# A four-layer graph network on one core: left-over rows on another queue, feature sums stored where they are made, entry counts moved by one sweep, and ties in the order of one queue

## The chip, the core and the metric

One core of a Trainium2 chip runs the whole program. The number that counts is the device time of one execution in microseconds (us); where runs are compared it is the median of several. Engines are named as the profile names them: PE is the matrix engine (PEld its weight loads), DVE the vector engine, ACT the scalar engine, POOL the general engine, SP the engine that here does nothing but issue transfers. A queue named SPq, ACTq or POOLq is the list of transfers that this engine issues, in order.

## The reference

A graph of 2708 nodes with 512 features and a dense matrix `adj` (2708 x 2708, float32, mostly zeros) goes through four layers. Each ends in a layer norm over the features:

```python
deg = jnp.maximum((adj != 0).sum(-1), 1.0)
x = layernorm(x + L0(x, adj))     # head = (adj > 0) / sqrt(count); inc = adj + head; (inc @ x) / sum(inc)
x = layernorm(x + L1(x, adj))     # gates from adj @ x; e = exp(-leaky_relu(s_left + s_right)) where adj != 0;
                                  # sigmoid(g_a * (e @ h) / sum(e) + g_b * (adj @ (x @ W) + b)), h = x @ W_sa
x = layernorm(x + L2(x, adj))     # x @ W0 + (A x) @ W1 + (A A x) @ W2 + (A A A x) @ W3
x = layernorm(x + L3(x, adj, deg))# relu((D^-1/2 (A + I) D^-1/2 x + x) @ W + b)
```

So `adj` is multiplied with a 2708 x 512 matrix seven times, in float32.

## The kernel before

**Seven sweeps over the matrix.** Each product with `adj` is one sweep. Sweep 0 is layer 0, sweep 1 makes `adj @ x` of layer 1, sweep 2 its attention product, sweeps 3 to 5 are the three hops of layer 2, and sweep 6 is layer 3. The nodes are split into two halves of 1354 and every sweep uses Strassen's seven block products (named P1 to P7 in sweeps 0 to 2, Q1 to Q7 in sweeps 3 to 6) on the blocks "11", "12", "21", "22" of the matrix and "B11" to "B22" of the features. The matrix blocks are combined by DVE (`comb`, line 419, and line 1382 in the later sweeps) into `s3` = 11 - 21, `s1` = 21 + 22, `s2` = s1 - 11, `s4` = 12 - s2; the feature blocks are combined into T1 to T4 (`x_sums` and `x_last`). Sweeps 0 to 2 go over four ranges of columns, 384, 384, 256 and 330 wide in sweeps 1 and 2; sweep 0 takes the 256 wide range first, as plain block products with no combining. Each half is ten blocks of 128 rows and 74 rows left over. `rest_adj` loads the left-over rows as a tile `r` of 116 rows and a tile `r32`, in which 32 rows stand four times.

**What sets the order.** The program is a list of pieces with positions: `at(pos, fn)` puts `fn` at a position, and the pieces are called in order of position. Sweep s begins at `S[s]` = 28 s, a range of sweeps 0 to 2 takes seven positions, and one position is one block product. From the list a scheduler then orders each engine's instructions by what it expects to be ready. A piece with `hold` keeps its place in the list, on all engines or on the one that is named. Until position 5 (`START`) the list holds throughout. [...]

**The pieces that the change touches.**

- *Start.* `count_mask` (lines 760 to 763) turns each matrix tile of the first range into zeros and ones, PE counts them (`cnt`, line 774), and a row `row` of one over the square root comes out (lines 795 to 814). `prep0` (lines 829 and 830) adds it to the tiles, and only then can the first product run. All loads of this range, `r` and `r32` among them, are on SP's queue.
- *Between sweeps 0 and 1.* `layernorm` has a step on POOL, a power (line 605), between two steps on DVE. Its result is stored to `X1` on POOL's queue and loaded again on POOL's queue as the features of sweep 1 (`next_x`, `x_load`, the loads at line 150).
- *Entry counts.* `extra1` counts the non-zero entries of each column for `deg`, tile by tile on DVE (`tally`, lines 1039 and 1042), in all four ranges of sweep 1. The counts lie in seven slots of one buffer, `masks`, which `sums2` later takes for weight sums.
- *Sweep 2's pairs.* `pairs2` finishes the nodes of a range during the next range, 128 nodes of both halves at a time: `b` is their dense product in two parts (`seven`, line 692), `c` a sigmoid on ACT, `e` the layer norm, `f` transposes both tiles (`ps_t`, line 642, `xT`), `z` makes the four sums S1 to S4 of the transposed tiles (`node_sums`, line 1193, names `d`), and `g` multiplies them. `f` and `g` hold their place on PE.
- *Added feature sums.* Sweep 3 multiplies features to the matrix's columns as two more blocks of rows. `ext_loads` loads the transposed features `X2T`, `ext_sums` (line 1344) makes their four sums on DVE and stores them to `SE` (`Es`, line 1345) on POOL's queue, in four parts for each of two column ranges g. Those of g = 0 run during sweep 2, at `S[2] + 19.3` and after, those of g = 1 during sweep 3. Their tiles come from the ring, 38 buffers that the matrix tiles, `e` tiles, sums and loads share.
- *Last sweep.* `done6` makes the dense product for finished columns (`row_sums`, line 682, then `seven`). `rest_add` (line 1519) adds the left-over rows' products `accr`, which take four of the eight accumulator banks.

Of the kernel before, what the change touches and what calls it, by code (L numbers as in the profile page):

```python
# [24 lines left out]
ALU = mybir.AluOpType  # L25
P = 128
EPS = 1e-5
NH = 1354
KT = 11
# [39 lines left out]
def gnn_kernel(ctx: ExitStack, tc: tile.TileContext, x, adjT, w_sa, a_sa, w_gcn, b_gcn, wab, bab, w_hop, w_out,  # L69
# [106 lines left out]
    events = []  # L176

    held = set()

    def at(pos, fn, hold=False):  # L180

# [68 lines left out]
    def x_load(src, k, s, eng):  # L250
# [2 lines left out]
        t = b12_tile(k) if s == "B12" else new_x(s, k)  # L253
        move(eng, t[:w], q)

    def next_x(base, src, sums=0.95, halves=-0.25):


        q = nc.gpsimd

        ql = nc.scalar if base == S[1] else q
        at(base + 1.3, lambda: rest_x(src, ql))
        for k in range(KW):
            f = k / KT
            if (k * P) < RANGES[-1][0]:
                at(base - 5.8 + f, lambda k=k: x_load(src, k, "B11", q))
                at(base - 1.85 + f, lambda k=k: x_load(src, k, "B22", q))
                at(base - 1.84 + f, lambda k=k: x_load(src, k, "B12", q))
                at(base + (0.03 if base == S[1] else -1.15) + f, lambda k=k: x_sums(k), True)
                at(base - 0.85 + f, lambda k=k: x_load(src, k, "B21", q))  # L270
                at(base + 1.5 + f, lambda k=k: x_last(k), True)
            else:
                at(base + halves + 0.05 * (k - 8), lambda k=k: x_load(src, k, "B22", ql))
                at(base + max(halves, 0.1) + 0.05 * (k - 8), lambda k=k: x_load(src, k, "B21", ql))
                at(base + sums + 0.03 * (k - 8), lambda k=k: x_sums(k), True)
                at(base + 2.6 + 0.03 * (k - 8), lambda k=k: x_last(k), True)
# [19 lines left out]
            rows_over(q, groups[s, "R"][0], (lo[:, c], hi[:, c]))  # L296
            q.dma_start(out=t32[64 * e : 64 * e + 64], in_=copies(hi[KA - KR :, c], 2))

    def rest_adj(h, R0, n):
        t, t32 = ring_tile("r"), ring_tile("r32")  # L300
        a = adjT[:, h * NH + R0 : h * NH + R0 + n]
        rows_over(nc.sync, t[:, :n], (a[NH - KR : NH], a[2 * NH - KR :]))
        nc.sync.dma_start(out=t32[:, :n], in_=copies(a[2 * NH - 32 :], 4))
        return t, t32

    REST_HOMES = [("B11", "B22"), ("B21", "T1")]
# [82 lines left out]
    def sweep(base, ranges, prep=None, extra=None, done=None, first=False, late=None, sums=False, save=False):  # L389
        A, spare = {}, {}  # L390
        nk = KW
        for r, (R0, n) in enumerate(ranges):
# [45 lines left out]
                        p, f = pw[ij]  # L438
                        at(pb + p + f * k / nk, lambda ij=ij, k=k, prepare=prepare: prepare(ij, k))

            def rest_load(h, R0=R0, n=n, r=r):
                A[r, "r", h], A[r, "r32", h] = rest_adj(h, R0, n)

            def rest_prepare(h, R0=R0, n=n, r=r):
                prep(R0, n, h, NT, KA, A[r, "r", h])
# [6 lines left out]
            for k in ks if not plain else ():  # L452
                f = 0.75 * k / nk
                at(pb + cw["s3"] + f, lambda k=k, comb=comb: comb("s3", "11", "21", ALU.subtract, k))
                at(pb + cw["s1"] + f, lambda k=k, comb=comb: comb("21", "21", "22", ALU.add, k))
                at(pb + cw["s2"] + f, lambda k=k, comb=comb: comb("11", "21", "11", ALU.subtract, k))
                at(pb + cw["s4"] + f, lambda k=k, comb=comb: comb("11", "12", "11", ALU.subtract, k))
                if sums:
                    at(pb + cw["s1"] + 0.95 + f, lambda k=k, run=run: run(1, k))
                    at(pb + cw["s4"] + 0.15 + f, lambda k=k, run=run: run(0, k))  # L460
# [137 lines left out]
    def layernorm(dsts, y, w, on_scalar=False, late=None):  # L598
        st = small.tile([P, 6], F32, name="st")
        nc.vector.bn_stats(st[:w], y[:w])  # L600
        mv = small.tile([P, 2], F32, name="mv")
        nc.vector.bn_aggr(mv[:w], st[:w])
        rstd = small.tile([P, 2], F32, name="rstd")
        nc.vector.tensor_scalar(rstd[:w, 0:1], mv[:w, 1:2], EPS, None, ALU.add)  # L604
        nc.gpsimd.tensor_tensor(rstd[:w, 1:2], rstd[:w, 0:1], neg_half[:w], ALU.pow)  # L605
        if on_scalar:
            nc.vector.scalar_tensor_tensor(rstd[:w, 0:1], mv[:w, 0:1], -1.0, rstd[:w, 1:2], ALU.mult, ALU.mult)
        for d, c0, c1 in dsts:
            if on_scalar:
                fn = lambda d=d, c0=c0, c1=c1: nc.scalar.activation(d[:w], y[:w, c0:c1], AF.Identity,  # L610
                                                                    bias=rstd[:w, 0:1], scale=rstd[:w, 1:2])
                fn() if late is None else late.append(fn)
                continue
            nc.vector.tensor_scalar(d[:w], y[:w, c0:c1], mv[:w, 0:1], rstd[:w, 1:2], ALU.subtract, ALU.mult)
# [414 lines left out]
    at(S[1] + 2.33 + 0.95 * (i - 1), scores_over)  # L1029

    def extra1(pb, r, R0, n, A):
        ts = tiles_of(R0, n)

        def tally(h, key, w=P):

            a = A[(r,) + key]
            if (R0, h) not in deg:
                deg[R0, h] = d = mask_tile()
                nc.vector.tensor_scalar(d[:w, :n], a[:w, :n], 0.0, None, ALU.not_equal)
            else:  # L1040
                d = deg[R0, h]
                nc.vector.scalar_tensor_tensor(d[:w, :n], a[:w, :n], 0.0, d[:w, :n], ALU.not_equal, ALU.add)  # L1042

        for ij, p in (("11", -0.6), ("21", 0.05), ("22", 1.05), ("12", 3.6)):
            for k in range(KW):
                at(pb + p + 0.8 * k / KT, lambda ij=ij, k=k: tally(int(ij[0]) - 1, (ij, k)), r == 0)
        for h, p in ((1, 2.0), (0, 4.5)):
            at(pb + p, lambda h=h: tally(h, ("r", h), KA))
            at(pb + p, lambda h=h: tally(h, ("r32", h), 32))

        def end(h):
            d = deg.pop((R0, h))
            ps = bank("ds", [P, 4])
            for i, q in enumerate(ts):
                wq = wt(q)
                nc.tensor.matmul(ps[:wq, i : i + 1], d[:, q * P - R0 : q * P - R0 + wq], ones_bf[:, 0:1], start=True,
                                 stop=True)
            for i, q in enumerate(ts):
                wq = wt(q)
                o = rdeg[:wq, h * KT + q : h * KT + q + 1]  # L1060
                nc.vector.tensor_scalar(o, ps[:wq, i : i + 1], 1.0, None, ALU.max)
                nc.vector.tensor_scalar(diag[:wq, h, q : q + 1], o, 1.0, None, ALU.add)
                nc.vector.reciprocal(o, o)

        def rows(h):
            to_rows(rdeg[:, h * KT + ts[0] : h * KT + ts[-1] + 1], len(ts),
                    DROW[h][0, ts[0] * P : (ts[-1] + 1) * P].rearrange("(k i) -> k i", i=P))

        at(pb + 2.6, lambda: end(1))
        at(pb + 3.7, lambda: rows(1))  # L1070
        at(pb + 5.2, lambda: end(0))
        at(pb + 6.3, lambda: rows(0))
# [78 lines left out]
            o, w = (W[2][2 * c + 1], w_sa) if k == 2 else (W[3][c][:, HD:], w_hop[3])  # L1151
            nc.scalar.dma_start(out=o, in_=w[c * P : (c + 1) * P, HD:])

    at(S[2] + 6.4, sums2)
    at(S[2] + 23.4, lambda: again(2))
    at(S[2] + 24.2, lambda: again(3))

# [9 lines left out]
    def extra2(pb, r, R0, n, A):  # L1167
# [7 lines left out]
        def share(o, s, t, w):  # L1175
            nc.vector.tensor_scalar(o, s, 1e-5, None, ALU.add)
            nc.vector.reciprocal(o, o)
            nc.vector.tensor_tensor(o, o, gate[:w, t, 0:1], ALU.mult)

        at(pb - 1.6, lambda: rows(0))  # L1180
        at(pb - 1.0, lambda: rows(1))
        at(pb + 5.2, lambda: run_sums(R0, n, 0, share))
# [2 lines left out]
    def node_sums(x, y):  # L1185
# [5 lines left out]
        for m, o, p, q, op in (("S3", r[0], a11, a21, ALU.subtract), ("S1", r[1], a21, a22, ALU.add),  # L1191
                               ("S2", r[2], r[1], a11, ALU.subtract), ("S4", r[3], a12, r[2], ALU.subtract)):
            nc.vector.tensor_tensor(o, p, q, op)
            Z.update({(m, c): o[:, c, :] for c in range(2)})
        for m, o in (("A11", a11), ("A12", a12), ("A22", a22)):
            Z.update({(m, c): o[:, c, :] for c in range(2)})
# [2 lines left out]
    def pairs2(p0, R0, n, C, tiles):  # L1199
        Y = {}  # L1200
        at(p0 + 0.2, lambda: Y.update(row_sums({(i, c): C[1 - i, c] for i in range(2) for c in range(DC)}, n)))
        for i, (t0, lo, w) in enumerate(tiles):
# [22 lines left out]
            def f(j, lo=lo, w=w, x1=x1, xT=xT):  # L1225
                v = transposed([(x1[j], 0, D)], w)
                for g, (i0, m) in enumerate(RANGES2):
                    c0, c1 = max(R0 + lo, i0), min(R0 + lo + w, i0 + 2 * m)
                    if c0 < c1:
                        store_T(X2T[g, 1 - j][:, c0 - i0 : c1 - i0], v[:, :, c0 - R0 - lo : c1 - R0 - lo])  # L1230
                xT.append(v)

            Z, G, o = {}, {}, []

            def z(Z=Z, xT=xT):
                Z.update(node_sums(*xT))

            def g(part, ts=ts, w=w, Z=Z, G=G, o=o):
                if part == 0:
                    o.extend(nat("y0") for _ in range(2))  # L1240
                seven(part, Z, W[10], G, 0, w, o, None, None)
                for j in range(2) if part else ():
                    move(nc.gpsimd, Y0[ts[j]], o[j][:w])

            p = p0 + 0.5 + 1.0 * i
            at(p - 0.25, a)
            at(p + 0.15, d)
            for j in range(2):
                at(p + 0.26 * j, lambda j=j, b=b: b(j))
                at(p + 0.45 + 0.02 * j, lambda j=j, e=e: e(j))  # L1250
                at(p + 0.84 + 0.06 * j, lambda j=j, f=f: f(j), nc.tensor)
                at(p + 1.22 + 0.22 * j, lambda j=j, g=g: g(j), nc.tensor)
            at(p + 0.4, c)
            at(p + 0.92, z)

    def done2(p0, dp, last, R0, n, h, C, tiles):
        if not last:
# [288 lines left out]


    for i in range(4):
        for g, p in enumerate((S[2] + 19.3 + 1.1 * i, S[3] + 6.6 + 1.3 * i)):
            a = ({}, g, i // 2, i % 2)  # L1550
            at(p, lambda a=a: ext_loads(*a))
            at(p + 0.5 + 0.6 * g, lambda a=a: ext_sums(*a))

    def hop_done(dst):

# [50 lines left out]
        for r in (64, 96):  # L1606
            nc.gpsimd.dma_start(out=diag_r[r : r + 32, 2:3], in_=d2[KA - KR : KR, KT - 1 :])

    at(S[2] + 4.0, diag_ends)

    def finish_degrees():
        t = small.tile([24, P], F32, name="fd", bufs=1)
# [26 lines left out]
    def done6(p0, dp, g, i0, n, h, cc, tiles):  # L1639

        end = (g, h) == (1, 0)
        def finish(s, lo, w, x, y):

            nc.vector.scalar_tensor_tensor(x[:w], y[:w], 0.0, x[:w], ALU.max, ALU.add)
# [80 lines left out]
    for n, i in enumerate(list(nc.cur_bb.bb.instructions)):  # L1725
# [5 lines left out]
        if n < strict:  # L1731
            last[i.engine] = i
        done[i.engine] = i


# [35 lines left out]
```

## Time and profile before

| | |
|---|---|
| median of 3 runs | 2843.36 us (2842.84 to 2844.38) |
| the profiled execution, its own time | 2845.44 us |
| span of its instructions | 2843.7 us |
| PE busy | 2802.4 us, 11550 matmuls |
| DVE busy | 2247.7 us |
| POOL busy | 617.2 us |
| mean granted clock of PE | 0.998 |

The page gives the busy time of each engine, the span in 40 slices, the chain of work that ended last, and groups of instructions by line. PE does not work in 41.3 us of the span. So the first question is not which engine is busy, but where these 41 us lie. They can be read from the timeline of PE, where each piece has in brackets the idle time before it and what ended that. About 1.7 us of an execution's own time lie outside the span of its instructions.

### The profile page before, as it was taken

What the parts mean: (1) busy time and instruction counts of PE and PEld (TensorE: products, weight loads), DVE (VectorE), ACT (ScalarE), POOL (GpSimd) and SP (SyncE); (2) the same over time, 40 slices, a digit from 0 to 9 for tenths busy, and PEclk for the clock granted to TensorE, in tenths of its full rate; (3) what the DMA queues carried; (4) which work ended last, traced back from release to release, by engine and by line L of the source; (5) the groups of instructions that cost most, each with busy time, mean ns of one, the idle gap of its engine ahead of it and who ended that gap; (6) DMA issues with size and microseconds to landing.
All of it is one profiled execution on the core that took longest, in us unless ns stands there. A gap on an engine that the chain in (4) does not pass through costs nothing.

```text
span 2843.7 us, 38764 instructions
## 1 busy us (share of the span) xinstructions
PE 2802.4 (99%) x11550; PEld 1939.7 (68%) x11550; DVE 2247.7 (79%) x5862; ACT 533.7 (19%) x1124; POOL 617.2 (22%) x1114
## 2 busy tenths in 40 slices
PE   7999999999999999999999999999999999999998
PEld 6899765658755667866666666666666666666665
DVE  6999699668737676775699778897888878899987
ACT  4644100101155353450100000000000100100001
POOL 0223223214310011223113033030330211601202
PEclk9999999999999999999999999999999999999999
DMA  8765476446534242665678667566675666854542
GB/s 234 241 195 184 140 228 218 150 131 196 189 92 139 78 152 69 203 194 158 205 205 255 192 208 234 163 210 203 197 235 173 189 194 180 243 167 146 179 142 90
DMA packets 370291, 511.72 MB, mean 180 GB/s; under 512 B 63632, under 2 KB 323460, under 8 KB 370080
## 3 DMA queue, kind: packets, MB, share of 16 engines
q1 hardware_dynamic: 303544, 371.61, 44.1%
q0 software_dynamic: 49376, 126.39, 13.3%
q10 hardware_dynamic: 17160, 11.24, 1.4%
q8 instruction: 92, 1.51, 0.2%
q14 instruction: 119, 0.97, 0.1%
HBM read 425.35 MB, written 83.66 MB: 179 GB/s over the span
## 4 chain that ended last, share of the span: by engine, by line
PE 86%; DVE 7%; issue 2%; DMA 1%; SPq 1%; ACT 1%; POOL 1%; POOLq 0%; DVEq 0%; ACTq 0%
PE accu L1437 12%; PE accd L1437 12%; PE accc L1437 12%; PE accu L489 7%; PE accd L489 7%; PE acca L1437 6%; PE ps L692 5%; PE accc L489 5%; PE acca L489 4%; PE accr L1508 2%; PE ps_d L653 2%; PE accd L475 2%; PE accc L475 2%; PE accu L475 2%; PE acca L475 1%
## 5 line engine op out<-in xcount | busy, mean ns | idle before, releaser
L1382 DVE TENSOR_TENSOR z<-z 128x339 f32<-128x339 f32 (+1 forms) x966 | 456.8, 507 | 10.9 <-PE accu L1437 2.9
L605 POOL TENSOR_TENSOR rstd<-rstd,neg_half 128x1 f32<-128x1 f32 (+3 forms) x91 | 61.2, 674 | 770.5 <-DVE rstd L604 484.0
L1455 ACT COPY q<-accu 128x338 f32<-128x338 f32 (+1 forms) x84 | 34.6, 443 | 996.5 <-PE accu L1437 836.2
L1437 PE MATMUL accc<-s,t 128*128 128x338 f32 (+1 forms) x644 | 198.1, 450 | 0.0
L1437 PE MATMUL accd<-z,t 128*128 128x338 f32 (+1 forms) x644 | 193.9, 448 | 1.4 <-DVE q L1519 1.4
L1437 PE MATMUL accc<-z,t 128*128 128x338 f32 (+1 forms) x644 | 193.5, 448 | 0.5 <-ACT q L1455 0.5
L1437 PE MATMUL accu<-z,t 128*128 128x338 f32 (+1 forms) x644 | 193.8, 448 | 0.0
L1570 POOL DMA_DIRECT2D Y<-y x192 | 104.8, 552 | 362.8 <-DVE y L1565 331.3
L419 DVE TENSOR_TENSOR a<-a,a 128x384 f32<-128x384 f32 (+2 forms) x330 | 164.2, 514 | 6.7 <-PE accu L489 5.5
L1437 PEld LDWEIGHTS accc<-s,t 128*128 128x128 f32 x644 | 120.9, 190 | 64.1 <-issue 7.5
L1437 PEld LDWEIGHTS accc<-z,t 128*128 128x128 f32 x644 | 122.0, 190 | 61.6 <-issue 1.0
L1437 PEld LDWEIGHTS accd<-z,t 128*128 128x128 f32 x644 | 121.9, 190 | 61.1 <-DVE q L1519 2.1
L1437 PEld LDWEIGHTS accu<-z,t 128*128 128x128 f32 x644 | 121.8, 190 | 59.9 <-issue 0.5
L1382 DVE TENSOR_TENSOR s<-z 128x338 f32<-128x338 f32 (+1 forms) x322 | 150.6, 506 | 9.1 <-PE accc L1437 7.7
L1461 DVE TENSOR_TENSOR q<-q,accd 128x338 f32<-128x338 f32 (+1 forms) x112 | 56.3, 503 | 122.4 <-PE accd L1437 122.4
L1163 ACT ACTIVATE e<-row,s_right 128x384 f32<-128x384 f32 (+5 forms) x176 | 95.7, 570 | 119.8 <-PE accc L489 28.5
L1165 DVE SCALAR_TENSOR_TENSOR a<-a,e 128x384 f32<-128x384 f32 (+2 forms) x160 | 77.0, 507 | 35.7 <-ACT e L1164 25.1
L1042 DVE SCALAR_TENSOR_TENSOR masks<-a,masks 128x384 bf16<-128x384 f32 (+2 forms) x152 | 76.0, 507 | 12.3 <-DMA a<-in_adjT 11.3
L422 POOL DMA_DIRECT2D As<-a x120 | 64.7, 542 | 88.3 <-DVE a L419 64.0
L829 DVE SCALAR_TENSOR_TENSOR s<-a,row 128x384 f32<-128x384 f32 (+2 forms) x152 | 75.8, 511 | 7.5 <-ACT row L814 7.5
L825 DVE TENSOR_TENSOR run<-run,a 128x384 f32<-128x384 f32 (+2 forms) x156 | 77.9, 499 | 1.4
L1164 ACT ACTIVATE e<-e 128x384 f32<-128x384 f32 (+5 forms) x176 | 78.7, 477 | 1.4
(787 smaller groups left out, 5957.6 us busy)
## 6 DMA issues: line engine op xcount, KB each, us to landing
z<-As SPq DMA_DIRECT2D x320, 169.5 KB
z<-As SPq DMA_DIRECT2D x320, 169.0 KB
a<-in_adjT SPq DMA_DIRECT2D x240, 192.0 KB
z<-in_adjT SPq DMA_DIRECT2D x240, 169.5 KB
z<-in_adjT SPq DMA_DIRECT2D x240, 169.0 KB
a<-in_adjT SPq DMA_DIRECT2D x120, 165.0 KB
a<-in_adjT SPq DMA_DIRECT2D x112, 128.0 KB
As<-a POOLq DMA_DIRECT2D x60, 192.0 KB, 3.5
```

The source lines that it names most:

```text
L419: nc.vector.tensor_tensor(A[r, dst, k][:, :n], A[r, a, k][:, :n], A[r, b, k][:, :n], op)
L475: nc.tensor.matmul(B[home, c][:, c0 : c0 + w], a[:, i * P : (i + 1) * P], x[:, d : d + w], start=bool(start and c0 == 0), stop=stop, skip_ ...
L489: nc.tensor.matmul(B[home, c][:, :n], X[STAT[p], k][:, c * P : (c + 1) * P], A[r, MOV[p], k][:, :n], start=bool(start and k == k0), stop=k ...
L692: nc.tensor.matmul(H[home][:w], Y[a, c][:, lo : lo + w], wop(v, c), start=part == 0 and home in "ud" and c == 0, stop=c == 1, skip_group_c ...
L825: nc.vector.tensor_tensor(run[R0, h][:w, :n], run[R0, h][:w, :n], t[:w, :n], ALU.add)
L1042: nc.vector.scalar_tensor_tensor(d[:w, :n], a[:w, :n], 0.0, d[:w, :n], ALU.not_equal, ALU.add)
L1163: nc.scalar.activation(e[:w, :n], row[R0, h][:w, :n], AF.Prelu, bias=s_right[:w, t : t + 1], alpha=0.01)
L1164: nc.scalar.activation(e[:w, :n], e[:w, :n], AF.Exp, scale=-1.0)
L1165: nc.vector.scalar_tensor_tensor(a[:w, :n], a[:w, :n], 0.0, e[:w, :n], ALU.not_equal, ALU.mult)
L1382: nc.vector.tensor_tensor(d[:, :n], Z[x + (k,)][:, :n], Z[y + (k,)][:, :n], op)
L1437: nc.tensor.matmul(B[home][:, :n], stat(v, k), a[:, :n], start=bool(start and k == 0), stop=k == nk - 1, skip_group_check=True)
L1570: nc.gpsimd.dma_start(out=rows[:, :, f * P : (f + 1) * P], in_=o[32 * f : 32 * (f + 1), : m * P].rearrange("p (b d) -> p b d", d=P))
```

## The change

Six things are changed. (1) In the first range of sweep 0 the tiles `r` and `r32` of the first half are loaded on POOL's queue. (2) The feature sums of g = 0 are no longer loaded back and made on their own. `z` of each pair, whose sums are the same values, stores them to `SE`; the two halves are given to `node_sums` in the other order for that, and half of one transposed store, which nothing reads any more, is left out. (3) The entry counts of the first range move from sweep 1 to sweep 2, and with them `diag_ends` and `sums2` to later positions. (4) The loads of sweep 1's features are tied behind the last power that stands ahead of them in the list (`behind_power`), so that POOL's order can't put them earlier; those of B21 move later in the list by 1.3 positions, some of B11 by half a position. (5) In `pairs2` the steps are moved apart by some hundredths of a position and `b` holds its place on PE; in the first range of sweep 1 `s1` holds its place on DVE. (6) In `done6` the finish of the first columns, (g, h) = (0, 0), comes 0.35 of a position later.

```diff
+    def behind_power(fn):
+        n = len(nc.cur_bb.bb.instructions)
+        fn()
+        if powers:
+            ties.extend((i, powers[-1]) for i in range(n, len(nc.cur_bb.bb.instructions)))
...
-                at(base - 5.8 + f, lambda k=k: x_load(src, k, "B11", q))
-                at(base - 1.85 + f, lambda k=k: x_load(src, k, "B22", q))
-                at(base - 1.84 + f, lambda k=k: x_load(src, k, "B12", q))
+                for s, p in (("B11", 5.8 - 0.5 * (base == S[1] and k > 2)), ("B22", 1.85), ("B12", 1.84)):
+                    at(base - p + f, lambda k=k, s=s: behind_power(lambda: x_load(src, k, s, q)))
                 at(base + (0.03 if base == S[1] else -1.15) + f, lambda k=k: x_sums(k), True)
-                at(base - 0.85 + f, lambda k=k: x_load(src, k, "B21", q))
+                at(base + (0.45 if base == S[1] else -0.85) + f, lambda k=k: (behind_power if base == S[1] else run_now)(
+                    lambda: x_load(src, k, "B21", q)))
...
-                A[r, "r", h], A[r, "r32", h] = rest_adj(h, R0, n)
+                A[r, "r", h], A[r, "r32", h] = rest_adj(h, R0, n, nc.gpsimd if plain and h == 0 else nc.sync)
...
-                at(pb + cw["s1"] + f, lambda k=k, comb=comb: comb("21", "21", "22", ALU.add, k))
+                at(pb + cw["s1"] + f, lambda k=k, comb=comb: comb("21", "21", "22", ALU.add, k),
+                   nc.vector if save and r == 0 else False)
...
         nc.gpsimd.tensor_tensor(rstd[:w, 1:2], rstd[:w, 0:1], neg_half[:w], ALU.pow)
+        powers.append(len(nc.cur_bb.bb.instructions) - 1)
...
     def extra1(pb, r, R0, n, A):
+        if r:
+            tallies(pb, r, R0, n, A, {"11": (-0.6, 0.8), "21": (0.05, 0.8), "22": (1.05, 0.8), "12": (3.6, 0.8)}, 2.0, 4.5)
...
-    at(S[2] + 6.4, sums2)
+    at(S[2] + 6.8, sums2)
...
+        if r == 0:
+            f = 1.0 * KT / KW
+            tallies(pb, r, R0, n, A, {"11": (-0.75, f), "21": (-0.15, f), "22": (1.0, 0.8 * f), "12": (3.45, f)}, 1.55, 3.95)
...
-                        store_T(X2T[g, 1 - j][:, c0 - i0 : c1 - i0], v[:, :, c0 - R0 - lo : c1 - R0 - lo])
+                        c = 2 if (g, j) == (0, 0) else 0
+                        store_T(X2T[g, 1 - j][c * P :, c0 - i0 : c1 - i0], v[:, c:, c0 - R0 - lo : c1 - R0 - lo])
...
-            def z(Z=Z, xT=xT):
-                Z.update(node_sums(*xT))
+            def z(lo=lo, w=w, Z=Z, xT=xT):
+                Z.update(node_sums(xT[1], xT[0]))
+                i0, m = RANGES2[0]
+                for s in range(2):
+                    c0, c1 = max(R0 + lo, i0 + s * m), min(R0 + lo + w, i0 + (s + 1) * m)
+                    for nm in SUMS if c0 < c1 else ():
+                        t = Z[nm.upper()]
+                        store_T(SE[nm, 0, s][:, c0 - i0 - s * m : c1 - i0 - s * m], t[:, :, c0 - R0 - lo : c1 - R0 - lo])
...
-                at(p + 0.26 * j, lambda j=j, b=b: b(j))
-                at(p + 0.45 + 0.02 * j, lambda j=j, e=e: e(j))
-                at(p + 0.84 + 0.06 * j, lambda j=j, f=f: f(j), nc.tensor)
-                at(p + 1.22 + 0.22 * j, lambda j=j, g=g: g(j), nc.tensor)
-            at(p + 0.4, c)
-            at(p + 0.92, z)
+                at(p + 0.3 * j, lambda j=j, b=b: b(j), nc.tensor)
+                at(p + 0.49 + 0.02 * j, lambda j=j, e=e: e(j))
+                at(p + 0.92 + 0.06 * j, lambda j=j, f=f: f(j), nc.tensor)
+                at(p + 1.38 + 0.22 * j, lambda j=j, g=g: g(j), nc.tensor)
+            at(p + 0.44, c)
+            at(p + 1.02, z)
...
-        for g, p in enumerate((S[2] + 19.3 + 1.1 * i, S[3] + 6.6 + 1.3 * i)):
-            a = ({}, g, i // 2, i % 2)
-            at(p, lambda a=a: ext_loads(*a))
-            at(p + 0.5 + 0.6 * g, lambda a=a: ext_sums(*a))
+        a, p = ({}, 1, i // 2, i % 2), S[3] + 6.6 + 1.3 * i
+        at(p, lambda a=a: ext_loads(*a))
+        at(p + 1.1, lambda a=a: ext_sums(*a))
...
-    at(S[2] + 4.0, diag_ends)
+    at(S[2] + 6.0, diag_ends)
...
+        if (g, h) == (0, 0):
+            p0 += 0.35
...
+    for i, j in ties:
+        tc.add_manual_dep(instructions[i], instructions[j].name,
+                          mybir.DependencyInfo(mybir.DependencyClass.NoSync, mybir.DependencyReason.DATA),
+                          reason="order of the list")
```

More of the change, by code (lines that the diff above doesn't have):

```diff
@@ L178, in gnn_kernel @@
     held = set()
+    powers, ties = [], []
     def at(pos, fn, hold=False):
@@ L254, in x_load, with run_now @@
         move(eng, t[:w], q)
+    def behind_power(fn):
[3 more added lines that the diff above has]
+            ties.extend((i, powers[-1]) for i in range(n, len(nc.cur_bb.bb.instructions)))
+    def run_now(fn):
+        fn()
     def next_x(base, src, sums=0.95, halves=-0.25):
@@ L297, in rest_x, with rest_adj @@
             q.dma_start(out=t32[64 * e : 64 * e + 64], in_=copies(hi[KA - KR :, c], 2))
-    def rest_adj(h, R0, n):
+    def rest_adj(h, R0, n, q=nc.sync):
         t, t32 = ring_tile("r"), ring_tile("r32")
         a = adjT[:, h * NH + R0 : h * NH + R0 + n]
-        rows_over(nc.sync, t[:, :n], (a[NH - KR : NH], a[2 * NH - KR :]))
-        nc.sync.dma_start(out=t32[:, :n], in_=copies(a[2 * NH - 32 :], 4))
+        rows_over(q, t[:, :n], (a[NH - KR : NH], a[2 * NH - KR :]))
+        q.dma_start(out=t32[:, :n], in_=copies(a[2 * NH - 32 :], 4))
         return t, t32
@@ L439, in sweep, with rest_load @@
                         at(pb + p + f * k / nk, lambda ij=ij, k=k, prepare=prepare: prepare(ij, k))
-            def rest_load(h, R0=R0, n=n, r=r):
-                A[r, "r", h], A[r, "r32", h] = rest_adj(h, R0, n)
+            def rest_load(h, R0=R0, n=n, r=r, plain=plain):
+                A[r, "r", h], A[r, "r32", h] = rest_adj(h, R0, n, nc.gpsimd if plain and h == 0 else nc.sync)
             def rest_prepare(h, R0=R0, n=n, r=r):
@@ L1031, in extra1, with tallies @@
     def extra1(pb, r, R0, n, A):
+        if r:
+            tallies(pb, r, R0, n, A, {"11": (-0.6, 0.8), "21": (0.05, 0.8), "22": (1.05, 0.8), "12": (3.6, 0.8)}, 2.0, 4.5)
+    def tallies(pb, r, R0, n, A, when, r1, r0):
         ts = tiles_of(R0, n)
@@ L1042, in tally @@
                 nc.vector.scalar_tensor_tensor(d[:w, :n], a[:w, :n], 0.0, d[:w, :n], ALU.not_equal, ALU.add)
-        for ij, p in (("11", -0.6), ("21", 0.05), ("22", 1.05), ("12", 3.6)):
+        for ij, (p, f) in when.items():
             for k in range(KW):
-                at(pb + p + 0.8 * k / KT, lambda ij=ij, k=k: tally(int(ij[0]) - 1, (ij, k)), r == 0)
-        for h, p in ((1, 2.0), (0, 4.5)):
+                at(pb + p + f * k / KT, lambda ij=ij, k=k: tally(int(ij[0]) - 1, (ij, k)))
+        for h, p in ((1, r1), (0, r0)):
             at(pb + p, lambda h=h: tally(h, ("r", h), KA))
@@ L1193, in node_sums @@
             nc.vector.tensor_tensor(o, p, q, op)
+            Z[m] = o
             Z.update({(m, c): o[:, c, :] for c in range(2)})
@@ L1242, in g @@
                 for j in range(2) if part else ():
-                    move(nc.gpsimd, Y0[ts[j]], o[j][:w])
+                    move(nc.gpsimd, Y0[ts[1 - j]], o[j][:w])
             p = p0 + 0.5 + 1.0 * i
@@ L1733, in gnn_kernel @@
         done[i.engine] = i
+    instructions = list(nc.cur_bb.bb.instructions)
+    for i, j in ties:
+        tc.add_manual_dep(instructions[i], instructions[j].name,
+                          mybir.DependencyInfo(mybir.DependencyClass.NoSync, mybir.DependencyReason.DATA),
+                          reason="order of the list")
 def kernel(x, adj, L1_gnn_W_sa, L1_gnn_a_sa, L1_gnn_W_gcnb, L1_gnn_b_gcnb, L1_gnn_Wa, L1_gnn_ba, L1_gnn_Wb,
```

## The prediction

> **What bounds the kernel now.** First the page, with busy time and share of each engine:
>
> ```profile
> span 2843.7 us, 38764 instructions
> PE 2802.4 (99%) x11550; PEld 1939.7 (68%) x11550; DVE 2247.7 (79%) x5862; ACT 533.7 (19%) x1124; POOL 617.2 (22%) x1114
> ```
>
> PE sets the time, and the change takes no matmul from it. So it can only win from PE's 41.3 us of idle time, or add to them. PE's timeline, read next, shows where they lie; brackets give the idle time ahead of a piece and what ended it.
>
> ```profile
> 20.49 5.16 PE L475 MATMUL acca<-B11A,a 128*128 128x256 f32 x12 [1.38 <-DVE a L830]
> ...
> 348.03 1.38 PE L489 MATMUL accd<-a,T1A 128*128 128x330 f32 x4 [0.69 <-DVE a L419]
> 350.51 2.49 PE L489 MATMUL accd<-a,T1A 128*128 128x330 f32 x8 [1.10 <-DVE a L419]
> ...
> 356.70 3.85 PE L489 MATMUL accd<-a,T1C 128*128 128x330 f32 x12 [1.48 <-DVE a L419]
> ...
> 1234.20 3.78 PE L692 MATMUL ps<-w,d 128*128 128x256 f32 x8 [3.36 <-DVE d L1193]
> 1237.77 3.65 PE L489 MATMUL accu<-a,T2A 128*128 128x330 f32 x8
> 1241.27 2.38 PE L489 MATMUL accc<-a,T4A 128*128 128x330 f32 x8
> ...
> 1256.71 0.63 PE L642 MATMUL ps_t<-ident,ld 128*128 128x128 f32 x4 [0.85 <-DVE ld L614]
> ...
> 2573.89 1.41 PE L1437 MATMUL accd<-z,t 128*128 128x338 f32 x4 [1.35 <-DVE q L1519]
> ...
> 2586.39 0.70 PE L692 MATMUL ps<-T2B,d 128*128 128x256 f32 x2 [0.80 <-DVE z L701]
> ```
>
> About 15 us pass before the first product at 20.49; 3.27 (0.69 + 1.10 + 1.48) go where sweep 1 begins; 4.21 (3.36 + 0.85) in sweep 2's last pairs; 2.7 in the last sweep (0.54 more at 2598). Some 7.4 at the end and a score of smaller gaps make the rest; the change doesn't touch the end. Then the queues. SP at the start, and two masks on DVE:
>
> ```profile
> 3.56 0.54 SPq L150 DMA_DIRECT2D r<-in_adjT  x1
> ...
> 5.50 0.64 SPq L303 DMA_DIRECT2D r<-in_adjT  x1
> 6.18 7.32 SPq L410 DMA_DIRECT2D a<-in_adjT  x14
> ...
> 10.55 0.29 DVE L760 TENSOR_SCALAR masks<-a 128x256 bf16<-128x256 f32 x1 [4.37 <-DMA a<-in_adjT]
> ...
> 16.07 0.29 DVE L760 TENSOR_SCALAR masks<-a 128x256 bf16<-128x256 f32 x1 [0.49 <-DMA a<-in_adjT]
> ```
>
> Fourteen matrix tiles stand behind the left-over rows; the seventh mask waits 4.37, and the first product comes 4.42 after the last mask. POOL at 346 and, from the waits (the numbers: sum in us, count, longest), who stood behind it; last a wait of ACT near 1223:
>
> ```profile
> 345.84 0.54 POOL L150 DMA_DIRECT2D B11B<-X  x1 [4.54 <-DMA X<-o]
> 346.39 0.56 POOL L605 TENSOR_TENSOR rstd<-rstd,neg_half 128x1 f32<-128x1 f32 x1
> ...
> DVE rstd L607 <- POOL rstd L605: 4.5, 3, 3.6
> ...
> ACT e L1163 <- DMA Es<-s: 4.1, 1, 4.1
> ```
>
> **What the Trainium skill says.** "Trainium Kernel Development and Optimization", Key Constraints: transfers of all queues share the same 16 DMA engines; issuing from several saves only issue time. So (1) is worth the 2.62 us between 3.56 and 6.18 first. "DMA: Bandwidth & Descriptors", Why a DMA increments its semaphore by 16 and not by 1: a transfer uses as many engines, at most 16, as divide both slowest dimensions. [...] The trace names no engines, but moved data fall to 30 GB/s in 6.0 to 7.5 us, between 169 and 238. "TensorE: Matmul & The Clock Gate", What's actually happening: an idle window of about 3.4 us halves PE's clock. The trace agrees: behind the 3.36 us gap the granted clock is 0.5 for 6.8 us, and eight 330 wide matmuls take 3.65 instead of 2.38 above. From start to start these eight lost 1.28 (3.50 against 2.22); with part of the eight before them I put the episode at 1.4.
>
> **The change part by part.**
>
> *(1) Start.* SP drops five issues, 2.62 us. POOL takes them behind the identity matrix, with no other work queued near them, so nobody waits for that; at 0.54 each they take it 2.7. Of the seventh mask's wait, 4.37, the issue is 2.62; the other 1.75 is transfer, which moves rather than goes. The later masks run at the pace of landing loads, and SP's next loads come forward too, so PE's small gaps between 48 and 56 (2.2), which hang on a second such pack of left-over rows, should stay as they are. I take **-3.0**; between -1.5 (the transfers collide on the engines) and -4.4 (the whole wait goes).
>
> *(4) Ties, and (5)'s hold in sweep 1.* A load that POOL ran early waited 4.54 for its own store `X`, and the power behind it came at 346.39. DVE was idle 342.9 to 347.0, 3.63 of it for that power, and is then over 23 of 28 us busy up to 476: PE's 3.27 is this delay handed on. In the new build POOL's order there is power, store, power, with the loads behind all. DVE then has 3.63 back against 3.27 needed. **-3.0**, between 0 (another wait there, say for ACT's rows) and -3.3. The loads of B12, B22 and B21 come later: B21's about 432 with landing at 442 to 445, and the tiles made of them are needed at 469; at least 10 us remain, and the part of B11 that moves by half a position keeps more. 0. The hold of `s1` only keeps DVE in the list's order, without work of its own: 0.
>
> *(3) Entry counts.* Forty tiles of the blocks and four of left-over rows: 44 DVE operations at a pitch of 0.47, 20.7 us. They leave sweep 1, where PE has no gap from 357 to 971: gain 0, hidden by PE's work. In sweep 2 some 32 of them (15.0 us) stand ahead of the last `s1`, ready at 875.5 and needed at 883.9; four `sums2` operations (1.3) leave. The window 840 to 868 has columns sum, then busy PE, PEld, DVE, ACT, POOL, then clock, DMA share, GB/s:
>
> ```profile
> 840.00:868.00 28.00, 28.00 (x90) 14.70 (x90) 15.50 (x34) 23.74 (x38) 2.20 (x4) 1.00 0.51 165
> ```
>
> DVE is idle for 12.5 of 28. 13.7 more against 8.4 of slack: 5.3 of the idle time must be usable. I take 0; at worst +3. The other 12 have 17 us, and `sums2`, issued near 925, is wanted at 954. `diag_ends` is four small transfers on POOL that only the last sweep needs: 0.
>
> *(2) Feature sums, and (5) in the pairs.* The 3.36 gap goes back over DVE to ACT, which waited 4.1 for a ring buffer that an `Es` store still read; the 0.85 stands behind such stores on POOL. The g = 0 loads (16, SP), sums (16, DVE) and stores (16, POOL) all vanish; half a transposed store vanishes too, and the halves' other order costs nothing, as the sums are the same number. Gone with them: 3.36 + 0.85 + the slow clock 1.4 = 5.6. Added: 28 stores of `z` tiles on POOL in the pairs of the first two ranges, 0.76 of issue each, 21 us spread over 170 in which POOL is mostly idle, landing in about 5.5 (median of both `Es` and `X2T` stores). In the built PE order some transposes stand closer, 1 matmul between instead of 3: +0.5. In two places such stores stand ahead of a power: +0.5 (0 to +3). **-4.6**; -6.6 if the pairs' other small gaps (1.5 near 1106 to 1127) go too, -2 if a gap stays that is only too short to halve the clock (1.4 + 0.6).
>
> *(6) Last sweep.* The built PE order now has the `accr` products ahead of the first dense product, so `accd` needn't wait for `rest_add`: 1.35 and part of 1.34 (0.80 + 0.54) go; but DVE is 24 to 27 of 28 busy there. **-1.6**; between -2.7 and +1.
>
> Sum: -3.0 - 3.0 - 4.6 - 1.6 = -12.2. On the profiled execution, 2845.44, that is 2833.2; the median is 2.1 lower, 2843.36, so **2831** there.
>
> **The rivals.**
>
> *Most likely, 0.68:* as summed, 2826 (ends near -17) to 2836.
>
> *Waits replaced, 0.18:* DVE has no room at 348 and at 2574, so (4) and (6) give nothing, and the start only 1.5. Its busy shares there speak for it; against it, that at 343 it idles. 1.5 + 4.6 = 6.1: 2837 (2834 to 2840).
>
> *POOL late, 0.07:* the stores ahead of the two powers hold these for 4 us (as at 345.84), and PE runs dry and halves its clock twice: 2 x (3.3 + 1.4) = +9.4 on the -12.2, 2840.6 (2838 to 2850). Against it: `z` tiles are complete before their stores' turn, whereas 4.54 was a wait for a landing.
>
> *Slower, 0.07:* each `z` tile now stays until its store has landed, up to 8.0 us. If the next pair's `e` or sums meet it as at 1223, an episode costs 5.6. From four of the six pairs it decides: 4 x 5.6 - 12.2 = +10, 2853. Against it: the 16 loaded tiles vanish from the ring, and pairs are a position, some 11 us, apart.
>
> That the ties change nothing is possible only for what POOL's order already had; then (4) is 0, as in the second case.
>
> **How the numbers follow.** 0.2%, 5.7 us, is about what a measurement of this kernel can tell from no change. Faster by more: all of the first case, 0.13 of the second, 0.01 of the third, 0.82. Within it: 0.05 of the second and 0.05 of the third, 0.10. Slower: 0.07 and 0.01, 0.08. The range goes from 2825.5 over the second case to 2839.
>
> **What the profile after would show.** First product at 17 to 18 and no mask wait over 3; powers near 342 with only stores between, no `accd` gap over 0.5 in the first 10 us of sweep 1; no PE gap over 1.5 in the pairs and the clock at 1.0 there; no gap for `rest_add`. DVE in 840 to 868 at 22 to 28 with PE still full. Wrong would be: a PE gap near 870 to 884, ACT or DVE waiting for `SE` stores, a first product after 19.

## The result, and the profile after

The changed kernel takes 2835.95 us (median of 8 runs, 2834.29 to 2836.70) against 2843.52 (8 runs, 2842.51 to 2844.41): a ratio of 0.9975, 95% interval 0.9965 to 0.9984, 7.6 us less. The forecast was 2831, with 2825.5 to 2839 as its range. The profiled execution took 2834.29, the fastest of the eight; that of before, 2845.44, is above all of its eight. So the two profiles lie 11.2 apart and the medians 7.6.

The page, first two lines:

```profile
span 2832.5 us, 38717 instructions
PE 2798.5 (99%) x11550; PEld 1937.8 (68%) x11550; DVE 2240.6 (79%) x5846; ACT 531.2 (19%) x1122; POOL 631.8 (22%) x1131
```

PE's timeline, at the places that were shown of before:

```profile
18.39 5.21 PE L487 MATMUL acca<-B11A,a 128*128 128x256 f32 x12 [1.38 <-DVE a L843]
...
350.56 3.85 PE L501 MATMUL accd<-a,T1C 128*128 128x330 f32 x12 [0.51 <-DVE a L430]
...
1154.64 1.10 PE L655 MATMUL ps_t<-ident,ld 128*128 128x128 f32 x8 [0.73 <-DVE y L712]
1167.70 0.60 PE L851 MATMUL rs<-ones_f,run 128*128 128x1 f32 x4 [0.63 <-DVE y L712]
...
1225.30 1.99 PE L705 MATMUL ps<-w,d 128*128 128x256 f32 x8
...
2574.46 0.70 PE L705 MATMUL ps<-T2B,d 128*128 128x256 f32 x2 [0.34 <-DVE z L714]
```

The 3.27 us near 350 are 0.51. The eight matmuls with `w` and `d` that came 3.36 late, and then took 3.78 at half the clock, take 1.99 with no wait. Of 1.35 and 0.80 in the last sweep 0.34 is left. New are, among others, 0.73 and 0.63 near 1155 and 1168.

How much each place gave is best read as a lead: the time at which PE has done the same amount of matmul work (columns streamed, counted from both traces), after minus before. A negative lead says that after is ahead. The heads of the columns are the work done, in us at full clock, which is within 50 us of the time itself. Steps of 0.3 or less mean nothing, as the two kernels' matmuls are not quite in the same order.

| | 100 | 380 | 470 | 900 | 1230 | 1300 | 2500 | 2850 | end of span |
|---|---|---|---|---|---|---|---|---|---|
| after | -2.85 | -6.14 | -5.96 | -5.72 | -5.65 | -13.06 | -13.03 | -14.66 | -11.2 |

So the start gave 2.9, the beginning of sweep 1 3.3, the pairs 7.4 and the last sweep 1.6. Some 0.5 was lost again in between, which leaves 14.7 us for PE. Then 3.5 were lost behind the last matmul, where the forecast had put nothing. The cause is found by asking for the instructions of the program's last line. Its drains stand behind all other work of each engine (duration in ns as least/median/most, first and last start in us). Of before:

```profile
L1767 POOLq DRAIN  x3: 46/102/3687, 2838.9 to 2843.4; - x3
L1767 SPq DRAIN  x3: 7/7/7, 2842.8 to 2843.1; - x3
```

and of after:

```profile
L1801 POOLq DRAIN  x3: 46/102/7445, 2824.2 to 2832.2; - x3
L1801 SPq DRAIN  x3: 7/7/7, 2828.0 to 2832.0; - x3
```

POOL's drain begins behind the last power. In before it ended at 2842.6, 0.2 ahead of SP, which had waited for the output's last store. In after it lasts 7.4 instead of 3.7 and ends at 2831.7, 3.7 behind SP's 2828.0. The kernel ends with it.

### The profile page after: what moved, and what is told of

Same layout as the page of the kernel before. It is cut to its first block, busy times and chain, and to the rows that moved or that the text cites. A ratio compares the mean times of both kernels' runs of the same rounds, so it can differ in the third digit from the quotient of the medians.

```text
span 2832.5 us, 38717 instructions
## 1 busy us (share of the span) xinstructions
PE 2798.5 (99%) x11550; PEld 1937.8 (68%) x11550; DVE 2240.6 (79%) x5846; ACT 531.2 (19%) x1122; POOL 631.8 (22%) x1131
## 3 DMA queue, kind: packets, MB, share of 16 engines
q0 software_dynamic: 49920, 125.95, 13.2%
## 4 chain that ended last, share of the span: by engine, by line
PE 88%; DVE 6%; DMA 2%; issue 2%; ACT 1%; SPq 1%; POOL 1%; POOLq 0%; ACTq 0%; DVEq 0%
PE accc L1465 12%; PE accu L1465 12%; PE accd L1465 12%; PE accd L501 7%; PE accu L501 7%; PE acca L1465 6%; PE accc L501 6%; PE ps L705 5%; PE acca L501 4%; PE accr L1536 3%; PE ps_d L666 2%; PE accd L487 2%; PE accc L487 2%; PE accu L487 2%; PE accr L1540 1%
```

## The experiments

In the comparisons that follow the kernel before took 2845.7 to 2847.3 us, so kernels are compared by the ratio to it. The leads are against the first profile of before, and their differences from one column to the next are what counts.

**The start alone** (before, with `rest_adj` of the first range on `nc.gpsimd`).

> The kernel before with part (1) alone: r and r32 of the first range on POOL's queue. Theory (each part of the gain stands on its own, in its own stage): first product near 18.4, PE 2.8 us ahead of before from there to its last matmul, so -2.8 us, less what POOL's last drain takes back. In the profile of before that drain takes 3.7 us and ends 0.3 before SP is ready, in the one of after it takes 7.4 and ends 3.6 behind SP. If it grows with the number of transfers POOL issued (1016 before, 1033 after, 1021 here), about 4.8 here and some 1 us lost; if it is chance, anything from 3 to 8. Rival (the start is caught up with at the next wait): first product near 18.4, but 0 by 350.

Ratio 0.9999 (0.9990 to 1.0007). The lead was 2.5 at 100 and 2.2 at 1230; behind 1230 it was 1.2. The stop there took more:

```profile
1233.31 3.78 PE L692 MATMUL ps<-w,d 128*128 128x256 f32 x8 [4.67 <-DVE d L1193]
```

The drain took 3.688 us, not 4.8. The start's gain is real, but in this profile 1.0 of it went at the next long stop. Two other kernels that keep that stop, the next one and the one with 17 transfers more, had 4.92 and 4.24 there without an earlier start, so this profile can't say whether the stop grew because PE came sooner.

**The ties and the hold of `s1` alone** (before, with `behind_power`, the later loads and the hold).

> The kernel before with part (4) and the hold of s1 alone. Theory: the power near 342 comes without a load ahead of it, the three gaps of 3.27 us where sweep 1 begins fall under 1, PE is 3.3 ahead of before at 380; POOL issues no more transfers than before, so its last drain stays at 3.7 and -3.3 us arrive. Rival (it was the entry counts' leaving that made room on DVE): the power comes early, but the gaps keep 2 us or more, and the time moves by less than 1.5 us.

Ratio 1.0004 (0.9996 to 1.0012), no gain. The lead at 330, 380 and 470 went from +0.7 to -1.7 and to +2.6: 2.4 were won where they were expected, and 4.3 lost some 60 us later, with the clock at half for 3.4 us. The profiled execution is one of the slowest of its thirteen, 3.1 us above their median, so 4.3 is a bad case:

```profile
354.97 3.85 PE L501 MATMUL accd<-a,T1C 128*128 128x330 f32 x12 [1.40 <-DVE a L430]
...
419.06 0.88 PE L649 MATMUL ps_n<-ident,P1c 128*128 128x128 f32 x2 [2.19 <-DVE P1c L576]
```

Neither theory had that: the power came early, the first gaps shrank from 3.27 to 1.40, and DVE, which was busy in 3.90 of the 4 us from 415 to 419, was late for the next thing.

**The entry counts back in sweep 1** (after, with the counts of (3) undone; `diag_ends` and `sums2` stay at their new positions).

> The kernel after with part (3) undone: the first range's entry counts are in sweep 1 again. Theory (no matmul waited for them at either place): the same within 1 us. Rival (DVE needs the 20.7 us in sweep 1): the gaps of 3.3 us near 350 come back, +2 to +4 us.

Ratio 0.9995 (0.9987 to 1.0004), while the kernel after, run beside it, had 0.9977 (next experiment). The lead went from -1.3 at 330 to -4.0 at 380 and back to -1.7 at 470. The lost 2.3 lie, as above, on results of DVE:

```profile
415.11 0.74 PE L649 MATMUL ps_n<-ident,P1c 128*128 128x128 f32 x2 [0.55 <-DVE P1c L576]
427.00 1.56 PE L501 MATMUL accu<-a,B11D 128*128 128x384 f32 x4 [1.03 <-DVE B11D L627]
```

DVE's busy time there, with the columns of the windows as before: first 364 to 476 of the kernel before, then the same stretch, 361 to 473, of after.

```profile
364.00:476.00 112.00, 112.00 (x410) 70.96 (x409) 106.16 (x301) 3.99 (x9) 39.87 (x71) 1.00 0.70 225
```

```profile
361.00:473.00 112.00, 112.00 (x405) 70.63 (x404) 93.77 (x296) 3.75 (x8) 42.33 (x77) 1.00 0.78 253
```

It is busy in 106 of 112 us, then in 94; in the kernel with the counts back it is 104. The other profiles bear it out: between 370 and 430 eight profiles with (4) and without these counts lost 0 to 1.6 us, the two with them 2.3 and 4.3. So (3) is what lets (4) keep most of its gain. The kernel with the counts back also stopped for 2.63 at 1162, with a halved clock, which is part of its slower time; why just there wasn't followed.

**The kernel after once more.**

> The kernel after, once more as it is. If POOL's last drain is given by what the kernel has issued, it takes 7.4 us again, within 0.5; if it is chance, it lies elsewhere between 3 and 8, and the spread of the times (2834.3 to 2836.7) is that of the drain.

Ratio 0.9977 (0.9967 to 0.9988). The drain took 7.443 us: given by the kernel, not by chance. PE's lead at the last matmul was 9.2 instead of 14.7. The lead at 100 was 1.4, not 2.9, with the first product at 19.21, and a gap of 0.63 was 1.96, where DVE waited for a buffer that a store to `SE` still read (the second line is a wait: sum in us, count, longest):

```profile
1172.09 0.61 PE L851 MATMUL rs<-ones_f,run 128*128 128x1 f32 x4 [1.96 <-DVE y L712]
```

```profile
DVE a L1182 <- DMA Es<-d: 2.1, 1, 2.1
```

So single executions differ by several us in waits for transfers, and the first profile of after was a good one.

**More transfers on POOL, the start undone, the stores on SP.** Three kernels on what the drain follows: before with 17 small loads on POOL's queue; after with `rest_adj(h, R0, n)` on SP; after with `store_T(SE[...], t[...], nc.sync)` in `z`.

> The kernel before with 17 more transfers on POOL's queue in sweep 4, each 16 rows of 4 bytes that nothing reads: POOL then issues 1033 in all, as in the kernel after, and with as many packets. Theory (the number of POOL's transfers, or of their packets, decides its last drain): the drain takes 7.4 us instead of 3.7, PE stays where it was, +3.5 us. Rival (it is the feature sums' stores themselves): the drain stays at 3.7 us, time the same within 0.5.

> The kernel after with part (1) undone: r and r32 are on SP's queue again, and POOL issues 1028 transfers. Theory on PE: first product 2 us later than in after, and up to 2.8 us stay to the last matmul (in part (1) alone, on before, 2.2 were left at 1230 and 1.1 behind the gap there, so the range is 1 to 2.8). Theory on the drain: if the step between 3.7 and 7.4 us lies above 1028, the drain falls to 3.7 and 3.6 us come back, so that the kernel is 1 to 2.5 us faster than after; if it lies between 1021 and 1028, or hangs on the stores, the drain stays at 7.4 and the kernel is 1 to 2.8 us slower.

> The kernel after with the 28 stores to SE that z makes on SP's queue instead of POOL's; POOL issues 1005 transfers. Theory (number of POOL's transfers): the last drain takes 3.7 us, SP ends the kernel, -3.6 us against after, if SP's loads are far enough ahead; the buffers that e * a waits for near 1170 come free as before or earlier. Rival (SP, which waits for z before it issues the next matrix loads, lets these come late): new PE gaps of 1 to 4 us in sweep 2 behind 970, which eat the gain.

Ratios 1.0004 (0.9996 to 1.0012), 0.9976 (0.9968 to 0.9985) and 1.0005 (0.9997 to 1.0014). The longest drain of each, from the same view as above:

| kernel | POOL's transfers | their packets | stores of the sums of g = 0 on POOL | drain, us |
|---|---|---|---|---|
| after, stores on SP | 1005 | 48704 | 0 | 1.65 |
| before | 1016 | 49376 | 16 | 3.69 |
| before, start alone | 1021 | 49648 | 16 | 3.69 |
| before, 17 loads more | 1033 | 49920 | 16 | 4.26 |
| after, start undone | 1028 | 49648 | 28 | 6.87 |
| after | 1033 | 49920 | 28 | 7.45 |

Neither the number of transfers nor that of packets decides: 1033 with 49920 has 4.26 and 7.45. With the 17 loads the rival was nearer, which had 3.7 against 7.4. The drain goes with the stores of the sums of g = 0: 1.65 without any, 3.69 and 4.26 with 16, 6.9 to 7.8 with 28 over all profiles; the 16 stores of g = 1 are on POOL's queue in all six. With the start undone the ratio is that of after, 0.9976 against 0.9977, and the first product comes at 20.6. Part (1) is not to be seen in the time, where each ratio is known to 0.001 (some 2.5 us), and neither size that was expected came.

With the stores on SP the drain is short and SP ends the kernel, yet PE stopped for 2.36 at 1049 and 5.84 at 1178, and its clock was at half for 10 us from 1175. The rival was right and its size too small. From 985 to 1180 SP's queue stood 62.3 us behind `d`, the sums of `z`, and DVE waited 6.5 for a matrix tile just ahead of the stop:

```profile
1177.59 1.01 PE L851 MATMUL rs<-ones_f,run 128*128 128x1 f32 x4 [5.84 <-DVE y L712]
...
SPq L744 <- DVE d L1213: 62.3, 13, 15.6
...
DVE a L1182 <- DMA a<-in_adjT: 6.5, 1, 6.5
```

**The last sweep undone** (after, without `p0 += 0.35`).

> The kernel after with part (6) undone. Theory: the waits for rest_add of before (1.35, 0.80 and 0.54 us near 2570 to 2600) are back, PE is 1.6 us later from there on, +1.6 us. Rival (the gaps went because the other parts moved DVE): the same within 0.5 us.

Ratio 0.9979 (0.9971 to 0.9986); a difference of 1.6 us is too small for these times. In the profile the lead stays at -10.66 from 2500 to 2850, where after gains 1.6, and the gaps are back as 1.35, 0.80 and 0.54. As the theory had it.

**No power behind POOL's last load** (after; in `layernorm` for the last columns and in `b_last`):

```diff
-        nc.gpsimd.tensor_tensor(rstd[:w, 1:2], rstd[:w, 0:1], neg_half[:w], ALU.pow)
+        nc.scalar.activation(rstd[:w, 1:2], rstd[:w, 0:1], AF.Sqrt)
+        nc.vector.reciprocal(rstd[:w, 1:2], rstd[:w, 1:2])
```

> The kernel after with the powers of the last six finishes (layernorm at the end of done6 and b_last) taken as a square root on ACT and a reciprocal on DVE, so that POOL has no work behind its last load near 2800. Theory (what the kernel after loses at its end is POOL's last drain, 7.4 us, begun only behind the last power at 2824): the drain starts near 2800 and ends some 20 us before SP is ready, SP sets the end, and the kernel is 3.0 to 4.5 us faster than after. Rival (the 3.6 us are a wait for something else that only looks like the drain): the end comes as far behind SP as in after, the same within 1 us.

The median is 2833.16 us, the ratio 0.9956 (0.9944 to 0.9969): 12.5 us faster than before and the fastest kernel here. From the start of the last matmul to the end of the span 6.8 us pass, against 11.2 in after and 7.7 in before. The drain is as long as ever and hidden:

```profile
L1806 POOLq DRAIN  x3: 46/102/7783, 2802.5 to 2831.1; - x3
L1806 SPq DRAIN  x3: 7/7/7, 2830.6 to 2830.9; - x3
```

It begins at 2802.5 and ends at 2810.3, 20 us before SP. Of the 4.4 us 3.7 are the drain's; the rest lies ahead of SP's last store, in the last finish. By the ratios this kernel is 5 to 6 us ahead of after, more than the end explains, but with five runs its interval still overlaps that of after.

**A second drain** (after, with `at(S[5] + 10, lambda: nc.gpsimd.drain(), nc.gpsimd)`; it stood at 2039 us, not at the place that the expectation gives).

> The kernel after with one more drain of POOL, near 1540 at S[5] - 18 + 28 of the list (in sweep 5, where POOL has pauses). Theory (the drain works off what earlier stores have left behind): the added one takes some us without hurting PE, the last one takes under 3.7 us, and the kernel is 2.5 to 4 us faster than after. Rival (the drain's length is a matter of the last transfers before it, or fixed for the program): the last one still takes 7.4 us and nothing is gained.

Ratio 0.9983 (0.9976 to 0.9989). The added drain took 7.3 us and the last one then 10.6. The theory fails: the earlier drain worked nothing off for the later one. The rival was right that nothing is gained, but had 7.4 for the last drain.

```profile
L1803 POOLq DRAIN  x3: 46/106/10623, 2827.1 to 2838.2; - x3
```

**The pairs alone** (before, with (2) and the steps of `pairs2`).

> The kernel before with part (2) and the pairs' part of (5) alone; POOL issues 1028 transfers, no left-over rows among them. Theory (the stop at 1230 with its halved clock goes, and the last drain grows with the 28 stores): PE 6 to 8 us ahead of before at 1300, of that 0.3 to 2 given up at 1155 to 1172, the drain at 6.9 us and 2.5 to 3 us of the gain lost at the end, so -3 to -5 us. Rival (PE's gain there needs the earlier start or the freed sweep 1): less than 3 us at 1300.

Ratio 0.9993 (0.9986 to 0.9999). The lead went from +1.0 at 1230 to -5.3 at 1300; 1.2 were lost at 2217 in a wait for ACT that after didn't have, and 2.9 at the end, where the drain took 6.87. The theory holds for PE, for the drain and for the loss at the end. The time moved by 2.9 at the medians and by some 2 us by the ratio, at or under the low end of the 3 to 5 that were expected.

**The new stores with the old steps** (the fastest kernel, with the steps of `pairs2` where before has them and `b` not held).

> The kernel g1_root (after, with the last six powers as root and reciprocal) with the steps of the pairs at their old positions and b not held on PE; the stores to SE stay in the pairs. Theory (part (2) makes the gain, the positions only shift small waits): still no halved clock near 1233 and PE 5 to 7 us further ahead of before at 1300 than at 1230, the total the same as g1_root within 1.5 us. Rival (the moved steps are what makes room for the stores): a stop of 2 us or more in the pairs and a total 3 us or more slower than g1_root.

Ratio 0.9969 (0.9959 to 0.9980) against 0.9956. By the profiles it is 8.8 us slower, but this one's execution was the slowest of its eight. The stop of before near 1233 is gone here too: PE's lead went from +6.2 at 1230 to -1.3 at 1300. Ahead of that it had gone from -3.5 at 990 to +6.2, with two stops that halved the clock. The third line is the stretch behind the first stop, all of it at a clock of 0.50.

```profile
1045.89 0.83 PE L855 MATMUL rs<-ones_f,run 128*128 128x1 f32 x6 [1.68 <-DVE y L716]
...
1172.88 0.95 PE L855 MATMUL rs<-ones_f,run 128*128 128x1 f32 x4 [2.67 <-DVE y L716]
...
1046.68:1050.10 3.42, 3.42 (x7) 1.89 (x7) 3.42 (x16) 0.54 (x2) 0.55 (x2) 0.50 0.56 180
```

From the waits of 960 to 1265:

```profile
ACT e L1184 <- DMA Es<-d: 7.8, 4, 4.5
...
DVE y L716 <- ACT y L733: 3.4, 2, 3.0
```

ACT's `e` stood 7.8 us behind buffers that the stores of `z` still read; in the kernel with the new steps it was 1.9. DVE's `y`, for which PE stopped, in turn stood 3.4 us behind ACT. The rival won on the stops; on the total, 0.13% or some 4 us between the ratios, it is ahead as well, though the two intervals overlap.

## Why the prediction was right, and where its steps were wrong

The gains came at the four places where they were forecast. That the time fell into the range is in part luck: at the medians 7.6 us came of some 12, and the errors below have both signs.

- **Start.** -3.0 forecast, -2.9 in the profile, with all 20 matrix tiles in one run on SP and the longest wait of a mask 1.17 instead of 4.37:

```profile
0.75 10.92 SPq L421 DMA_DIRECT2D a<-in_adjT  x20
```

```profile
9.55 3.59 DVE L773 TENSOR_SCALAR masks<-a 128x256 bf16<-128x256 f32 x11 [1.17 <-DMA a<-in_adjT]
```

  The agreement is closer than the reasoning deserves. At the first product only 2.1 are won, 18.39 against 20.49. The other 0.8 are smaller gaps between 48 and 56, of which the forecast said that they should stay as they are; they are smaller with the start undone, too. Over all profiles here the first product comes at 17.98 to 19.64 with (1) (nine profiles) and at 20.49 to 21.24 without (five), 2.2 apart in the mean. Two of the nine, the second of after among them, are later than 19, which the prediction had named as a sign of being wrong. The 2.2 fit what the Trainium skill says ("Trainium Kernel Development and Optimization", Key Constraints), that issuing from several queues saves issue time: 2.62 of it were taken from SP. No comparison of times shows the gain.

- **Sweep 1.** -3.0 forecast, -3.3 found. The power no longer has a load ahead of it:

```profile
DVE rstd L620 <- POOL rstd L617: 1.4, 3, 0.5
```

  What failed is the step that put the entry counts at "gain 0, hidden by PE's work". PE had no gap behind 357 because it had been late just before. With the ties alone DVE, at 106 of 112 us in the kernel before, passed the delay on to 415 to 427. Beside (4), (3) is worth about 2 to 4 us; no run has it alone.

- **Entry counts in sweep 2.** The forecast 0 holds: the lead is -5.96 at 470 and -5.72 at 900, and PE is full in 840 to 868 with DVE 3.2 us busier:

```profile
840.00:868.00 28.00, 28.00 (x86) 15.12 (x85) 18.68 (x39) 22.20 (x37) 2.20 (x4) 1.00 0.57 174
```

  DVE was to be at 22 to 28 in this stretch. It is not, as many of the counts ran ahead of it, from 799 on.

- **Pairs.** -4.6 forecast (to -6.6), -7.4 found. The term that was mis-sized is the slow clock, 1.4: of the sixteen matmuls behind the stop the first eight took 3.57 from start to start, against 1.83 in after, and the next eight lost 1.28 more: 3.0 together. 3.36 + 0.85 + 3.0 = 7.2. This agrees with the half clock of the Trainium skill ("TensorE: Matmul & The Clock Gate", What's actually happening): PE worked 6.1 of the 6.8 us at half clock, and lost half of that. Its idle window of about 3.4 us, which the prediction took over, is not the least that halves the clock here: a single stop of 1.68 did, with the old steps, while 1.96 in the second profile of after and 2.36 with the stores on SP did not.

  In eight profiles with the new stores and steps, the stop and what hung on it gave 6.3 to 7.4 from 1228 to 1300. The costs set against it, 1.0 together, took 0.1 from 960 to 1228 in the first profile of after, 0.2 to 2.0 in six others and 4.6 with the counts back. In the second profile of after DVE waited 2.1 us for an `SE` store, which the prediction had also named as a sign of being wrong.

  The old steps show what the moved ones are for: the stop near 1233 goes without them too, but the slower rival's mechanism, buffers held by stores of `z`, comes in two places.

- **Last sweep.** -1.6 forecast and found, and gone without its edit.

- **The end.** "The change doesn't touch the end" was the wrong step: POOL's drain behind the last power grew from 3.7 to 7.4 us and ended the kernel. Two errors in opposite directions, +3.5 there and -2.8 in the pairs, left the profile's sum at -11.2 against -12.2. The rest to the median's -7.6 is that the two profiles stood at the good and the bad end of their runs. With the drain hidden the fastest kernel has the forecast's 12 us.

The rival of 2837 gave nearly the measured number for reasons that didn't happen: sweep 1 and the last sweep did give back what they had.

## What to carry to other kernels

DVE, busy at 95%, hid nothing here: where a wait ahead of such an engine is removed, price what it will be late for next, and treat work that leaves it as part of the same edit. A gap that halves PE's clock costs the gap and again half of the slow time, here 3.36 and 3.0 us. Read what a change gives from more than one profile. Look at the drains behind the last store, and let an engine that has issued many stores finish early: with no work for POOL in the last 30 us its drain cost nothing.

## What was not expected of the hardware

POOL's last drain took from 1.65 to 7.78 us without a second one. In after it took 7.443 and 7.445, though it began 24 us after POOL's last transfer was issued; begun together with that transfer, in the fastest kernel, it took 7.78. It grew with the stores of the feature sums on POOL's queue and not with the number of transfers or packets alone, and with an earlier drain of 7.3 us it took 3.2 longer. What it does in that time stays open.

The clock of PE was at half behind single stops of 1.68 and 2.19 us, and at full behind others of 1.96 and 2.36. What decides between them wasn't looked for.
